# Sums over keys by block transposes on VectorE and one small matmul, in a two-layer graph network

## The chip, the cores and the metric

The kernel runs on one core of a Trainium2 chip, and the metric is the device time of that core in microseconds: the median of several executions. A core has five engines, each with its own queue of instructions, executed in order: TensorE (PE, the matrix multiplier; PEld in the profile is its loading of stationary operands), VectorE (DVE), ScalarE (ACT), GpSimd (POOL) and SyncE (SP), which issues the transfers to and from DRAM here. [...] PE writes to PSUM, of which the kernel keeps eight buffers of one bank each, and DVE and ACT empty them.

## The reference

Two layers over x of shape (64, 256, 512), in float32, with one adjacency matrix `adj` of 256 x 256.

```python
# layer 0: attention with 8 heads of 64, masked by adj
q = (x @ Wq + bq).reshape(b, n, H, HD)      # k and v alike
scores = einsum('bqhd,bkhd->bhqk', q, k) / sqrt(HD)
scores = scores + (1.0 - adj)[None, None, :, :] * -1e9
attn = softmax(scores, axis=-1)
out = einsum('bhqk,bkhd->bqhd', attn, v).reshape(b, n, d)
x = layernorm(x + out @ Wo + bo)
# layer 1: graph attention with one head
h = x @ W
s1, s2 = h @ a1, h @ a2
e = leaky_relu(s1[:, :, None] + s2[:, None, :], 0.2) * adj
att = softmax(e, axis=2)
x = layernorm(x + elu(att @ h + beta * h))
```

## The kernel before

The 64 batches are worked in 32 pairs. q, k and v of a pair are projected together, with seven products in place of eight (Strassen's scheme: `project`, whose matmuls all lie on line 437 and write the PSUM tiles `ps_chain`, `ps_cross`, `ps_second`, `ps_fourth` or `ps_pair`). The rest runs batch by batch; s = 0 or 1 is the batch in its pair. In the order of a batch the stages are:

- *scores*: for each of four head pairs c, four matmuls with 64 rows each into two PSUM tiles `ps_sc` (line 756). They hold keys on the partitions and queries along the row. DVE adds the mask (line 763), ACT takes the exponential without subtracting a maximum (765), giving `pT`, and POOL adds the two key halves into `both` (768).
- *sums*: the softmax denominators are sums over keys, thus over partitions. `denominators` does them with eight matmuls against a strip of ones into `ps_den` (781), takes the reciprocal on DVE (798), and lets ACT sum denominators and reciprocals into `range_sb` (794). The reciprocals go to DRAM as eight rows (806), and two transfers spread them over the partitions of `inv_all` (810).
- *mix*: the exponentials times v, into `ps_pv` (733). ACT copies it to `oT`, and DVE multiplies by `inv_all` (836).
- *o*: the output projection, added to x (914), with operands `oS` that POOL prepares (408); then the layer norm (569 to 586).
- *logits*: DVE's products with `wa_sb` (937), a small block transpose, a trip of one row through DRAM, and the masked softmax of layer 1 (966 to 986).
- *attention*, *spread*, *u*: the attention is transposed through DRAM and DVE (1003 to 1010), applied to the normed x (`X_sums`, `att_sums` prepared by POOL at 1046), the result `yT` (483) multiplied by W, then ELU (697 to 700), the second norm and the store (704).

Which stage of which pair PE works at when is written out by hand. `ROUND` is the order in one round, `LATER` says how many rounds after its own a stage of a pair comes, and `FINISH` is the order of the last stages. The class `Plan` takes all operations with assumed durations and dependences, gives PE's operations due times from that order (with `SWITCH` ns whenever the array's shape, `mode`, changes), and places the other engines' operations by greedy planning against those due times. What comes out is the fixed order of each engine's queue. `slots` says how many buffers of each kind there are.

At the end the check at line 1085 looks whether every value in `range_sb` is at most `SAFE` = 1e15. If not, a second, general path recomputes everything; with these inputs it isn't taken.

Of the kernel before, what the change touches and what calls it, by code (L numbers as in the profile page):

```python
# [22 lines left out]
ROUND = ("sums1", "mix1", "scores0", "spread1", "v", "u1", "attention0", "sums0", "mix0", "scores1", "o1", "x",  # L23
         "logits1", "q", "spread0", "o0", "attention1", "u0", "k", "logits0")

LATER = {"x": -2, "q": -1, "k": -1, "v": 0, "scores0": 0, "scores1": 0, "sums0": 0, "sums1": 1, "mix0": 0, "mix1": 1,
         "o0": 0, "o1": 1, "logits0": 0, "logits1": 1, "attention0": 1, "attention1": 1, "spread0": 1, "spread1": 2,
         "u0": 1, "u1": 2}

FINISH = (("sums1", 1), ("mix1", 1), ("scores0", 0), ("v", 0), ("attention0", 1), ("spread1", 2), ("sums0", 0), ("u1",  # L30
          2), ("mix0", 0), ("scores1", 0), ("o1", 1), ("logits1", 1), ("o0", 0), ("attention1", 1), ("u0", 1),
          ("spread1", 1), ("logits0", 0), ("spread0", 1), ("sums1", 0), ("mix1", 0), ("attention0", 0), ("spread0",
          0), ("o1", 0), ("attention1", 0), ("u1", 1), ("u0", 0), ("logits1", 0), ("spread1", 0), ("u1", 0))
# [25 lines left out]
class Plan:  # L59
# [11 lines left out]
    SWITCH = 250.0  # L71
# [161 lines left out]
def gnn_two_layers(ctx: ExitStack, tc: tile.TileContext, x, adj, Wq, bq, Wk, bk, Wv, bv, Wo, bo, W, a, beta, out):  # L233
# [13 lines left out]
    slots = {"xin": 2, "x": 4, "two": 6, "xP": 1, "piece": 6, "full": 4, "half": 18, "xS": 2, "st": 76, "ps": 8, "rows": 4, "svT": 4, "line": 4, "square": 4}  # L247
# [83 lines left out]
    range_sb = once([2, B], "range_sb")  # L331
# [348 lines left out]
    def batch(m, s, qT, kT, V, dram, general):  # L680
# [59 lines left out]
        def attention_by_keys():  # L740
# [3 lines left out]
            inv, everywhere = sb("half", [N], "inv"), sb("full", [C, N], "inv_all")  # L744
            rows = Buf(dram_pool, "rows", [H, N], "rows")

            def scores(c):

                turn("scores")
# [11 lines left out]
                for i in range(2):  # L761
# [5 lines left out]
                    if not last:  # L767
                        plan.op("POOL", 725, lambda h=h, i=i: nc.gpsimd.tensor_tensor(  # L768
                            both[c][:, i, :], pT[h][:, 0, :], pT[h][:, 1, :], ALU.add),
                            [pT[h]], [(both[c], i)])  # L770

            def denominators():
                turn("sums")

                acc = ps([N], "ps_den")

                def pe():
                    for k in range(NT if last else 1):
                        for i in range(2):
                            for c in range(C):  # L780
                                nc.tensor.matmul(  # L781
                                    acc[32 * c:32 * c + 32, :], ones[:, 16 - 16 * i:48 - 16 * i],
                                    pT[2 * c + i][:, k, :] if last else both[c][:, i, :],
                                    start=i == 0 and k == 0, stop=i == 1 and (k == NT - 1 or not last))

                if last:
                    plan.op("PE", 1500, pe, pT, [acc], mode="sums", claims=[inv])
                else:
                    plan.op("PE", 1000, pe, both, [acc], mode="sums", claims=[inv])

                def sum_of(i, src):

                    junk = sb("half", [N], "junk")
                    plan.op("ACT", 600, lambda: nc.scalar.activation(  # L794
                        junk[A], src[A], AF.Identity, accum_out=range_sb[:, i, b:b + 1]), [src],
                        [junk, (range_sb, (i, b))])

                plan.op("DVE", 1750, lambda: nc.vector.reciprocal(inv[A], acc[A]), [acc], [inv])  # L798
                for i, d in enumerate((acc, inv)):
                    sum_of(i, d)  # L800
                if last:
                    select = sb("half", [H, HD], "select")
                    plan.op("DVE", 690, lambda: nc.vector.tensor_copy(
                        select[A], ident[:, 0:P:P // H].unsqueeze(2).to_broadcast([P, H, HD])), [acc], [select])
                    return [spread_last(select, inv, g) for g in range(2)]
                plan.op("SP", 500, lambda: nc.sync.dma_start(rows[A], inv[0:P:P // H, :]), [inv], [rows])
                for i in range(2):
                    def spread(i=i):
                        r = rows[A]
                        nc.sync.dma_start(everywhere[i * HD:(i + 1) * HD], bass.AP(  # L810
                            tensor=r.tensor, offset=r.offset + i * N, ap=[[0, HD], [2 * N, C], [1, N]]))

                    plan.op("SP", 1000, spread, [rows], [(everywhere, i)])
# [29 lines left out]
            spread_inv = denominators()  # L843
# [3 lines left out]
        def attention_by_queries():  # L847
# [5 lines left out]
            def scores(t, g):  # L853
                turn("scores")
# [227 lines left out]
    fine, row, least = st(1, "fine"), ps([P], "row"), st(1, "least")  # L1082
    ok = sb("half", [2, B], "ok")

    def check():
        nc.vector.tensor_scalar(ok[A], range_sb[A], SAFE, None, ALU.is_le)
        nc.vector.tensor_reduce(fine[A], ok[A], AX.XY, ALU.min)

    plan.op("DVE", 500, check, [range_sb], [ok, fine])
# [53 lines left out]
```

## Time and profile before

| | |
|---|---|
| Time, median of 3 runs | 2719.87 us (2719.57 to 2720.87) |
| Span of the profiled execution, first to last instruction | 2718.3 us |
| Mean granted TensorE clock | 0.997 |
| Instructions | 47307 |
| A pair of batches in the middle (1033.98 to 1117.62) | 83.64 us |
| Transfers | 300.79 MB, 111 GB/s |

The profiled execution has a span of 2718.3 us; the runs that are timed are 1.6 us above that, for what lies around the span. In a line of the profile, L781 is line 781 of the kernel; `ps_den<-both,ones` is what is written and read; "x64 | 112.5, 1758 | 18.5" are the count, the busy time in microseconds, the mean length of one in nanoseconds, and the time that the engine stood idle just before these instructions. Lengths of instructions that follow each other overlap by their latencies, so their sum is above the busy time. A float32 matmul is recorded as two.

### The profile page before, as it was taken

What the parts mean: (1) busy time and instruction counts of PE and PEld (TensorE: products, weight loads), DVE (VectorE), ACT (ScalarE), POOL (GpSimd) and SP (SyncE); (2) the same over time, 40 slices, a digit from 0 to 9 for tenths busy, and PEclk for the clock granted to TensorE, in tenths of its full rate; (3) what the DMA queues carried; (4) which work ended last, traced back from release to release, by engine and by line L of the source; (5) the groups of instructions that cost most, each with busy time, mean ns of one, the idle gap of its engine ahead of it and who ended that gap; (6) DMA issues with size and microseconds to landing.
All of it is one profiled execution on the core that took longest, in us unless ns stands there. A gap on an engine that the chain in (4) does not pass through costs nothing.

```text
span 2718.3 us, 47307 instructions
## 1 busy us (share of the span) xinstructions
PE 2696.2 (99%) x15919; PEld 2268.6 (83%) x15919; DVE 1956.4 (72%) x3677; ACT 1548.9 (57%) x3713; POOL 1721.8 (63%) x2254
## 2 busy tenths in 40 slices
PE   9999999999999999999999999999999999999997
PEld 7888888888888888888888888888888888888886
DVE  6777677777777677777767777777767777776766
ACT  3455556556556565565555655655656556555566
POOL 5756666665666656666666666566665666666654
PEclk9999999999999999999999999999999999999998
DMA  8434434344443444434443434444344443443221
GB/s 245 103 100 123 121 96 117 96 121 125 99 121 86 119 129 106 106 104 105 125 119 98 115 95 125 125 98 120 88 120 129 106 107 104 104 126 103 83 70 45
DMA packets 579056, 300.79 MB, mean 111 GB/s; under 512 B 404864, under 2 KB 509816, under 8 KB 578808
## 3 DMA queue, kind: packets, MB, share of 16 engines
q1 hardware_dynamic: 578680, 297.68, 41.4%
q8 instruction: 130, 2.13, 0.3%
q14 instruction: 118, 0.97, 0.1%
q0 software_dynamic: 128, 0.01, 0.0%
HBM read 245.11 MB, written 52.48 MB: 109 GB/s over the span
## 4 chain that ended last, share of the span: by engine, by line
PE 97%; DVE 1%; POOL 0%; ACT 0%; issue 0%; DMA 0%; SPq 0%; ACTq 0%; POOLq 0%; DVEq 0%
PE ps_chain L437 33%; PE ps_cross L437 22%; PE ps_pair L437 10%; PE ps_sc L756 8%; PE ps_pv L733 8%; PE ps_second L437 6%; PE ps_fourth L437 6%; PE ps_den L781 2%; DVE junk L543 0%; DMA xin<-in_x_dram 0%; ACT junk L569 0%; DMA row<-line 0%; SPq L631 0%; PE ps_y L1021 0%; PE ps_plain L502 0%
## 5 line engine op out<-in xcount | busy, mean ns | idle before, releaser
L768 POOL TENSOR_TENSOR both<-pT 128x256 f32<-128x256 f32 x504 | 354.6, 731 | 383.1 <-ACT pT L765 383.1
L763 DVE TENSOR_TENSOR pT<-ps_sc,maskT_sb 128x512 f32<-128x512 f32 x512 | 324.0, 680 | 85.4 <-PE ps_sc L756 85.4
L765 ACT ACTIVATE pT<-pT 128x512 f32<-128x512 f32 x512 | 304.0, 625 | 52.3 <-DVE pT L763 49.7
L937 DVE SCALAR_TENSOR_TENSOR junk<-x,wa_sb 128x512 f32<-128x512 f32 x256 | 206.8, 833 | 109.4 <-ACT x L586 108.2
L756 PE MATMUL ps_sc<-qT,kT 64*128 64x256 f32 x2048 | 238.4, 382 | 0.0
L733 PE MATMUL ps_pv<-pT,v 128*64 128x256 f32 x2048 | 235.1, 382 | 0.0
L756 PEld LDWEIGHTS ps_sc<-qT,kT 64*128 64x128 f32 x2048 | 192.8, 187 | 44.4 <-issue 24.6
L474 ACT COPY u<-ps_chain 128x256 f32<-128x256 f32 x126 | 46.9, 372 | 318.4 <-PE ps_chain L437 318.2
L586 ACT ACTIVATE x<-x,nmr,rs 128x512 f32<-128x512 f32 x256 | 197.5, 808 | 44.7 <-POOL nmr L582 44.6
L733 PEld LDWEIGHTS ps_pv<-pT,v 128*64 128x64 f32 x2048 | 141.4, 137 | 91.0 <-DVE kT L483 12.8
L1046 POOL TENSOR_TENSOR X_sums<-x 128x256 f32<-128x256 f32 x126 | 151.6, 1213 | 100.1 <-ACT x L586 98.6
L569 ACT ACTIVATE junk<-x,mean 128x512 f32<-128x512 f32 x256 | 182.2, 714 | 3.8 <-DVE mean L575 3.6
L569 ACT ACTIVATE junk<-x 128x512 f32<-128x512 f32 x256 | 159.4, 625 | 38.6 <-DVE x L914 31.8
L717 POOL TENSOR_TENSOR x<-x,res_sb 128x512 f32<-128x512 f32 x128 | 175.7, 1374 | 0.0
L580 POOL TENSOR_SCALAR rs<-sq 128x2 f32<-128x2 f32 (+1 forms) x130 | 34.8, 268 | 208.8 <-ACT junk L569 203.5
L408 POOL TENSOR_TENSOR oS<-oT 128x256 f32<-128x256 f32 x126 | 92.2, 731 | 86.7 <-DVE mean L575 53.0
L836 DVE TENSOR_TENSOR oT<-oT,inv_all 128x512 f32<-128x512 f32 x126 | 132.7, 1091 | 0.0
L975 POOL TENSOR_TENSOR e<-e,adj_sb 128x512 f32<-128x512 f32 (+1 forms) x66 | 82.2, 1247 | 77.0 <-DVE e L972 77.0
L437 PE MATMUL ps_chain<-so_sb,oS 128*128 128x256 f32 x504 | 129.3, 379 | 0.0
L437 PE MATMUL ps_chain<-sw_sb,yS 128*128 128x256 f32 x504 | 129.2, 379 | 0.0
L798 DVE RECIPROCAL inv<-ps_den 128x256 f32<-128x256 f32 x64 | 112.5, 1758 | 18.5 <-ACT junk L794 9.3
L408 POOL TENSOR_TENSOR yS<-yT 128x256 f32<-128x256 f32 x126 | 91.8, 729 | 51.7 <-DVE yT L483 31.8
(242 smaller groups left out, 7162.7 us busy)
## 6 DMA issues: line engine op xcount, KB each, us to landing
x<-in_x_dram SPq DMA_DIRECT2D x64, 512.0 KB
out_dram<-x SPq DMA_DIRECT2D x128, 256.0 KB
inv_all<-rows SPq DMA_DIRECT2D x126, 256.0 KB
xin<-in_x_dram SPq DMA_DIRECT2D x248, 128.0 KB
wq_sums<-wq_sums SPq DMA_DIRECT2D x124, 256.0 KB
wk_sums<-wk_sums SPq DMA_DIRECT2D x124, 256.0 KB
wq_sums<-in_L_gnn_Wq_dram SPq DMA_DIRECT2D x93, 256.0 KB
wk_sums<-in_L_gnn_Wk_dram SPq DMA_DIRECT2D x93, 256.0 KB
```

Source lines behind the costliest of these rows:

```text
L408: plan.op("POOL", 180 + 545 * width // P, lambda: nc.gpsimd.tensor_tensor(dst(), p(), m(), ALU.subtract), reads, writes)
L437: nc.tensor.matmul(dst[:, f, :], lhs, rhs, start=start and f == 0 and c == 0, stop=c == inner - 1, skip_group_check=True)
L569: plan.op("ACT", 700, lambda: nc.scalar.activation(junk[A], X[:, t, :], func, bias=mean[:, i:i + 1] if bias else 0.0, accum_out=to[:, i:i ...
L586: plan.op("ACT", 810, lambda i=i, t=t: nc.scalar.activation(X[:, t, :], X[:, t, :], AF.Identity, bias=nm[:, i:i + 1], scale=rs[:, i:i + 1] ...
L717: plan.op("POOL", 1270, lambda t=t: nc.gpsimd.tensor_tensor(X[:, t, :], X[:, t, :], res_sb[A], ALU.add), [res_sb], tokens(t))
L733: nc.tensor.matmul(acc[r * HD:(r + 1) * HD, i, :], V[:, 2 * k + s, h * HD:(h + 1) * HD], pT[h][:, k, :], start=k == 0, stop=k == NT - 1)
L756: nc.tensor.matmul(acc[j][:, k, :], kT[r:r + HD, c, key_blk(k)], own(qT, r, c), start=True, stop=True)
L763: plan.op("DVE", 690, lambda h=h, i=i: nc.vector.tensor_add(pT[h][A], acc[i][A], maskT_sb[A]), [acc[i], maskT_sb], [pT[h]])
L765: plan.op("ACT", 620, lambda h=h: nc.scalar.activation(pT[h][A], pT[h][A], AF.Exp, scale=1.0 / HD ** 0.5), [pT[h]], [pT[h]])
L768: plan.op("POOL", 725, lambda h=h, i=i: nc.gpsimd.tensor_tensor(both[c][:, i, :], pT[h][:, 0, :], pT[h][:, 1, :], ALU.add), [pT[h]], [(bot ...
L937: plan.op("DVE", 780, lambda t=t, i=i, junk=junk: nc.vector.scalar_tensor_tensor(junk[A], X[:, t, :], 1.0, wa_sb[:, i, :], op0=ALU.mult, o ...
L1046: plan.op("POOL", ns, lambda: nc.gpsimd.tensor_tensor(dst(), p(), m(), op), reads, writes)
```

## The change

The sums over keys get another form in all batches but the last. `both[c]` (keys of one half on 128 partitions, two heads, 256 queries) is transposed on DVE in blocks of 32 x 32 into `flip`, and a reduction along 32 elements leaves in `part` the sum of each block of 32 keys, with the query modulo 32 on the partition. After the four head pairs, one matmul with `part` as the stationary operand (64 columns: 8 heads by 8 groups of 32 queries) and `fold_sb` (four unit matrices of 32 x 32 stacked, made once) as the moving one adds the four blocks of keys. It leaves the denominators as 64 x 32. Their reciprocals, now 32 columns instead of 256, go to one row of a DRAM tile `rows_all` that keeps all batches; the spreading transfers read from there.

ACT's two summing passes go, with `range_sb`. Instead the end reads `rows_all` back once and compares the reciprocals with `SAFE` and 1/`SAFE` in four passes on DVE. The last batch keeps the matmuls against ones and gets its own comparison.

`ROUND`, `LATER` and `FINISH` are written anew: sums now come after the mix, and the four head pairs of the scores are stages of their own. `SWITCH` becomes 100. There is one `half` buffer fewer, and `flip`, `part` and `inv` have one buffer each.

```diff
-ROUND = ("sums1", "mix1", "scores0", "spread1", "v", "u1", "attention0", "sums0", "mix0", "scores1", "o1", "x",
-         "logits1", "q", "spread0", "o0", "attention1", "u0", "k", "logits0")
+ROUND = ("mix1", "sums1", "scores30", "scores20", "scores00", "scores10", "logits0", "v", "spread1", "o1", "u1", "x",
+         "mix0", "sums0", "scores31", "scores21", "scores01", "scores11", "attention0", "q", "attention1", "logits1",
+         "k", "spread0", "o0", "u0")
...
-    SWITCH = 250.0
+    SWITCH = 100.0
...
-    slots = {"xin": 2, "x": 4, "two": 6, "xP": 1, "piece": 6, "full": 4, "half": 18, "xS": 2, "st": 76, "ps": 8, "rows": 4, "svT": 4, "line": 4, "square": 4}
+    slots = {"xin": 2, "x": 4, "two": 6, "xP": 1, "piece": 6, "full": 4, "half": 17, "flip": 1, "part": 1, "inv": 1,
+             "xS": 2, "st": 76, "ps": 8, "rows": 4, "svT": 4, "line": 4, "square": 4}
...
-    range_sb = once([2, B], "range_sb")
+    rows_all = Buf(dram_pool, "rows_all", [B - 1, H * N], "rows_all")
...
+    fold_sb = once([32], "fold_sb")
+    plan.op("DVE", 150, lambda: nc.vector.tensor_reduce(
+        fold_sb[A], ident.rearrange("p (b j) -> p j b", j=32), AX.X, ALU.add), [], [fold_sb])
...
-                turn("scores")
+                turn(f"scores{c}")
...
+                if last:
+                    return
+                turned = sb("flip", [2, N], "flip")
+                plan.op("DVE", 640, lambda: nc.vector.transpose(turned[A], both[c][A]), [both[c]], [turned])
+                plan.op("DVE", 600, lambda: nc.vector.tensor_reduce(
+                    part[:, 2 * c:2 * c + 2, :], turned[A].rearrange("p i (q k) -> p i q k", k=32), AX.X, ALU.add),
+                    [turned], [(part, c)])
...
+                acc, inv = ps([32], "ps_den"), sb("inv", [32], "inv")
+                plan.op("PE", 130, lambda: nc.tensor.matmul(
+                    acc[0:P // 2], part[A].rearrange("p h q -> p (h q)"), fold_sb[A], start=True,
+                    stop=True), [part, fold_sb], [acc], mode="columns", claims=[inv])
+                plan.op("DVE", 280, lambda: nc.vector.reciprocal(inv[0:P // 2], acc[0:P // 2]), [acc], [inv])
+                spread_rows(lambda r: r.rearrange("(p q) -> p q", q=32), lambda: inv[0:H * N // 32], inv)
+
+            def spread_rows(to, src, inv):
+                plan.op("SP", 500, lambda: nc.sync.dma_start(to(rows_all[b]), src()), [inv], [(rows_all, b)])
+                for i in range(2):
+                    def spread(i=i):
+                        r = rows_all[b]
+                        nc.sync.dma_start(everywhere[i * HD:(i + 1) * HD], bass.AP(
+                            tensor=r.tensor, offset=r.offset + i * N, ap=[[0, HD], [2 * N, C], [1, N]]))
+
+                    plan.op("SP", 1000, spread, [(rows_all, b)], [(everywhere, i)])
...
-                def sum_of(i, src):
-
-                    junk = sb("half", [N], "junk")
-                    plan.op("ACT", 600, lambda: nc.scalar.activation(
-                        junk[A], src[A], AF.Identity, accum_out=range_sb[:, i, b:b + 1]), [src],
-                        [junk, (range_sb, (i, b))])
...
+                def in_range():
+                    nc.vector.tensor_scalar(ok[:, 0, :], inv[A], SAFE, None, ALU.is_le)
+                    nc.vector.tensor_scalar(ok[:, 1, :], inv[A], 1.0 / SAFE, None, ALU.is_ge)
+                    nc.vector.tensor_reduce(last_ok[A], ok[A], AX.XY, ALU.min)
...
+    plan.op("SP", 1000, lambda: nc.sync.dma_start(
+        flat(kept), bass.AP(tensor=rows_all[A].tensor, offset=rows_all[A].offset, ap=[[n, P], [1, n]])), [rows_all],
+        [kept])
...
+        nc.vector.tensor_scalar(flat(ok), flat(kept), SAFE, None, ALU.is_le)
+        nc.vector.tensor_scalar(flat(kept), flat(kept), 1.0 / SAFE, None, ALU.is_ge)
+        nc.vector.tensor_tensor(flat(ok), flat(ok), flat(kept), ALU.mult)
+        nc.vector.tensor_reduce(fine[:, 0:1], flat(ok), AX.X, ALU.min)
+        nc.vector.tensor_tensor(fine[:, 1:2], fine[:, 0:1], last_ok[A], ALU.mult)
```

In the instruction order that the planner makes of this, each round on PE is: mix and sum, scores, v, spread, o, u; then mix and sum, scores, q, k, spread, o, u. Before, it was: sum, mix, scores, spread, v, u; then sum, mix, scores, o, q, spread, o, u, k.

## The prediction

> **What bounds the kernel now.** I read four views, in the order in which one rules the next out. First the profile's page: the engines' busy time and the chain that ended last.
>
> ```profile
> span 2718.3 us, 47307 instructions
> PE 2696.2 (99%) x15919; PEld 2268.6 (83%) x15919; DVE 1956.4 (72%) x3677; ACT 1548.9 (57%) x3713; POOL 1721.8 (63%) x2254
> PE 97%; DVE 1%; POOL 0%; ACT 0%; issue 0%; DMA 0%; SPq 0%; ACTq 0%; POOLq 0%; DVEq 0%
> ```
>
> TensorE (PE) is 99% of the span and 97% of the chain. A busy PE could still be a slow PE, so I read the waits of PE next (microseconds in total, times, longest).
>
> ```profile
> PE tr_x L620 <- DMA xin<-in_x_dram: 4.3, 2, 3.7
> PE ps_chain L437 <- ACT attT L999: 1.5, 1, 1.5
> PE tr_a L996 <- DVE rc L983: 1.4, 1, 1.4
> ```
>
> These are the largest, and all lie in the first or the last 50 us. Between them PE waits for nobody. So a microsecond taken from PE's queue comes off the end one for one, and work on another engine is free until it makes PE wait. Third, PE's timeline around one sum over keys (start, length, line, count):
>
> ```profile
> 1115.68 1.03 PE L437 MATMUL ps_chain<-sw_sb,yS 128*128 128x256 f32 x4
> 1116.64 1.07 PE L781 MATMUL ps_den<-both,ones 128*32 128x256 f32 x16
> 1117.64 3.67 PE L733 MATMUL ps_pv<-pT,v 128*64 128x256 f32 x32
> 1121.25 3.73 PE L756 MATMUL ps_sc<-qT,kT 64*128 64x256 f32 x32
> 1124.90 1.13 PE L437 MATMUL ps_chain<-wo_sb,oT 128*128 128x256 f32 x4
> ```
>
> Lengths overlap, so I use starts. The sum L781 holds PE from 1116.64 to 1117.64: 1.00 us. Four full-size products are 0.864 us apart elsewhere, so 1115.68 + 0.864 = 1116.54: the change of array shape before the sum costs 0.10 us. Fourth, the sum over one pair of batches, in the stretch view (length, then busy time of PE, PEld, DVE, ACT, POOL):
>
> ```profile
> core 0: us, PE busy (x) PEld busy (x) DVE busy (x) ACT busy (x) POOL busy (x), PEclk, DMA share, GB/s
> 1033.98:1117.62 83.64, 83.64 (x500) 70.61 (x496) 60.64 (x114) 48.28 (x117) 53.68 (x70) 1.00 0.44 112
> ```
>
> A pair takes 83.64 us, all of it PE at full clock, with DVE (VectorE) at 60.6.
>
> **The change, part by part.**
>
> *The sum on PE.* Its 8 matmuls leave 63 of 64 batches: 63 x 1.00 = 63.0 us. In their place stands one matmul with 64 stationary columns and 32 moving ones. The trace shows none so small. It shows every f32 matmul as two instructions (1008 in 63 x 8), and these weight loads:
>
> ```profile
> L733 PEld LDWEIGHTS ps_pv<-pT,v 128*64 128x64 f32 x2048 | 141.4, 137 | 91.0 <-DVE kT L483 12.8 <-issue 12.7 <-DVE v L483 0.8
> L756 PEld LDWEIGHTS ps_sc<-qT,kT 64*128 64x128 f32 x2048 | 192.8, 187 | 44.4 <-issue 24.6
> ```
>
> Nothing hides a load of 64 columns behind a multiply of 32, so the nearest row gives 2 x 137 = 274 ns. The Trainium skill (TensorE: Matmul & The Clock Gate, section "LDWEIGHTS (loading the stationary operand)") prices a load by its columns alone, P/1.2 ns: 53 ns, twice 107. The rows explain the gap: 64 to 128 columns cost 50 ns more, 0.8 a column, as the rule says, over a fixed 85 ns which the rule leaves out. By the row the sum is 63 x (1.00 - 0.274) = 45.7 us saved, by the rule 56.3. The fixed part is mostly overlapped in streams (128-column products follow each other at 0.11 us though their loads last longer), so I take 0.15, nearer the rule: 63 x 0.85 = **53.6 us saved**.
>
> *Shape changes.* Before: full, sum, mix, scores, full: four changes. After, the instruction order is mix, sum, scores in every round, and a 64-column output has the mix's shape: three. The change that goes is already inside the 1.00 us; the 0.10 in front stays, now in front of the mix. No further credit. The planner's SWITCH of 100 instead of 250 and the new ROUND only set this order.
>
> *ScalarE.* Two summing passes a batch go (383 + 194 + 417 + 192 ns, 76 us in all) from an engine at 57% that PE never waits for: nothing. POOL's work stays.
>
> *VectorE.* Mean rows that bear on it:
>
> ```profile
> L798 DVE RECIPROCAL inv<-ps_den 128x256 f32<-128x256 f32 x64 | 112.5, 1758 | 18.5 <-ACT junk L794 9.3 <-PE ps_den L781 9.2
> L1010 DVE STREAM_TRANSPOSE attT<-att_b 128x512 f32<-128x512 f32 x62 | 43.5, 702 | 0.1
> L977 DVE TENSOR_REDUCE nm<-e 128x2 f32<-128x512 f32 x62 | 41.9, 675 | 1.1 <-POOL e L975 1.1
> L836 DVE TENSOR_TENSOR oT<-oT,inv_all 128x512 f32<-128x512 f32 x126 | 132.7, 1091 | 0.0
> ```
>
> Added per batch: 4 transposes and 4 reductions of 128x512, 4 x (0.702 + 0.675) = 5.5 us. Removed: 1.76 of reciprocal, which on 32 columns costs some 0.35 (from 165 ns at 2 columns, 6.3 ns each more). Net +4.1 a batch, +8.2 a pair: DVE goes from 60.6 to 68.8 of about 81.9 us. This is hidden only while DVE, whose queue is in order, clears PSUM and the operands in time, so I walk the tighter half of the new order: scores, v, spread, o, u, mix, sum, about 35 us on PE (the half with q and k has 47). Products' lengths come from starts in PE's timeline: v 12.10, spread 3.15, o and u 6.05 each. DVE's instructions there, at mean durations: masks 8 x 0.68, new ones 5.5, v adds 4 x 0.68, logits 3 x 0.91, the two L836 2.2, transpose 0.7, adds for y, x, u 16 x 0.42, rest (logits' softmax, ELU, statistics) 8.8: 34.8 us. Queued instructions overlap by 7% (16 masks of 680 ns take 10.1 us in a pair): 32.4, or 93% of the half. Tight, but not over.
>
> Walk, t = 0 at the scores: PE has v from 3.75 to 15.85, spread to 19.0, o to 25. DVE: reciprocal, transpose, eight masks with one add between to 6.9; transpose and reduction to 8.1 (the transpose waits for POOL's sums of two exponentials, whose masks are done at 4.5; 0.6 on ScalarE and 2 x 0.73 on POOL make 6.6, in time); waits for v's third product (9.1); v add, logits, to 11.5; L836 twice to 13.7; v add, transpose, reduction, transpose to 16.3; two v adds to 17.6; the y add at 17.95. PE's sixth spread product (18.1) waits for that add: a slack of about 0.1 us. In o a similar place comes out 0.1 late. Each late moment shifts PE and gives DVE the time back, so I take 0.15 us a pair, 31 pairs: **5 us lost**, from 0 to the case below. L836 is what moves it: behind it in the queue stand the v adds, and for them PE.
>
> *Reciprocals through DRAM.* The same 8 KB a batch in 64 pieces of 128 B instead of 8 of 1 KB; the two spreading transfers are the same, and on SP's queue they follow the write at once in one half as before (1119.59 to 1121.47), in the other they stand between weight fetches. In the tight half L836 comes 11.5 us after the sum. Reciprocal 0.45, write to the end of the spread's issue 3.2 as before (1119.59 to 1122.76), and landing at most 4.5 (in one half issued by 1099.94, with L836 at 1104.48): 8.2, hidden. Without that cover L836 waits, and behind it the v adds, for which PE's banks wait. SBUF has one `half` buffer fewer; 0.
>
> *End.* The range check is now one 516 KB read on SP between the last spread and the last batches' logit and attention transfers, which need their data only a round later, then four passes of 1008 columns on DVE: by slopes between 256 and 512 columns 2 x 0.72 + 1.19 + 1.18 + 0.3 = 4.1 us, plus 1.4 for the last batch's own. They stand ahead of the two copies of the last y, for which the last projection waits. DVE has holes there (3.9 us at 2680): between 0 and 5.5, I take **2 us lost**.
>
> Sum: 2718.3 - 53.6 + 5 + 2 = 2671.7 us of span. The runs' median is 1.6 above the span (2719.87 against 2718.3), the same program frame around it: **2673 us**.
>
> **Rivals.**
>
> *A, nothing is lost:* the small matmul costs the rule's 0.107, the two other terms are 0. 2718.3 - 56.3 + 1.6 = 2663.6. For it: PE never waited for DVE in a round. Against: 93%. Chance 0.17, 2655 to 2667.
>
> *B, POOL holds DVE up:* The Trainium skill (SBUF — State Buffer, section "SBUF: two separate sides") says a DVE instruction with two SBUF inputs and a POOL instruction exclude each other for their whole length. The new transposes and reductions have one input, and their rows are steady (673 to 711 ns), but L836 has two: median 684, mean 1091, longest 1761. Mean price: my walk. With both at the longest, the y add is 1.3 us later, in every pair: 31 x 1.3 = 40 us, 2718.3 - 53.6 + 40 + 2 + 1.6 = 2708. For it: the round repeats, so a collision repeats. Against: the median is the free one. Chance 0.19, 2684 to 2714.
>
> *C, DVE becomes the bound (slower):* one mechanism, DVE's queue in the tight half (scores to sum). Without overlap (34.8), with both L836 at the longest and the waits for PE in the walk (3), it lasts 39.1 against 35: 4.1 a pair, 127 us, 2795. It decides from (53.6 - 2)/31 = 1.7 us a pair. Against: it needs all of DVE's instructions at their dearest. Chance 0.04.
>
> *D, the small matmul is no gain:* if it drained the array on both sides and so cost as much as the eight, 1 us, with nothing else lost: 2720. Against: it has the mix's shape, and measured shape changes are 0.10. Chance 0.02.
>
> **The numbers.** My forecast, 0.58, has its own range 2662 to 2684. The wide range, 2658 to 2698, holds it, most of A and half of B. A measurement tells 0.2% (5.4 us). Faster: forecast, A and B, and of C the little below 1.7 us a pair: 0.95; same, most of D: 0.015; slower, the rest of C and D: 0.035.
>
> **What would show it.** The sum's start to the scores' start after the mix: mix 3.6 plus 0.15. A pair at 82 us; PE waits for DVE in spread or o of 0 to 0.3 us a pair; DVE near 83% of the span; the last products a few us after where their work alone would put them. I am wrong if the small matmul takes over 0.3 us, if PE waits on v's or y's adds by more than 0.5 us a pair, or if the end waits for the range check.

## The result, and the profile after

The kernel after takes 2688.94 us (median of 4 runs, 2687.40 to 2692.57) against 2719.90 us for the kernel before beside it. The ratio is 0.9889 with a 95% interval of 0.9875 to 0.9903: faster by 1.1%. The forecast was 2673.0, so the sign was right, the wide range held it, and 16 of the expected 47 us did not come. It fell outside the likeliest case's own range (2662 to 2684) and into the band of rival B. The profiled execution was the slowest of the four (2692.57; span 2690.8), 27.5 us of span below the one of before.

The page of the kernel after: engines and the chain that ended last.

```profile
span 2690.8 us, 45707 instructions
PE 2662.2 (99%) x15037; PEld 2252.2 (84%) x15037; DVE 2212.4 (82%) x4188; ACT 1483.6 (55%) x3457; POOL 1688.5 (63%) x2254
PE 97%; DVE 1%; DMA 0%; issue 0%; ACT 0%; POOL 0%; SPq 0%; POOLq 0%; DVEq 0%
```

PE is still 99% of the span. DVE rose from 72% to 82%. The time at PE's own place is seen in its timeline around the new small matmul (start, length, line, count), and the cost of a pair of batches in the stretch view, the whole pair first and then its two halves, the one with v and the one with q and k.

```profile
1111.11 1.13 PE L448 MATMUL ps_chain<-sw_sb,yS 128*128 128x256 f32 x4
1112.17 3.67 PE L744 MATMUL ps_pv<-pT,v 128*64 128x256 f32 x32
1115.67 0.25 PE L794 MATMUL ps_den<-fold_sb,part 128*64 128x32 f32 x2
1115.85 1.35 PE L767 MATMUL ps_sc<-qT,kT 64*128 64x256 f32 x10
```

```profile
1080.18:1162.80 82.62, 82.55 (x471) 70.07 (x469) 68.51 (x132) 46.24 (x108) 52.47 (x71) 1.00 0.42 112
1080.18:1115.85 35.67, 35.60 (x208) 29.59 (x206) 31.49 (x60) 20.01 (x47) 26.62 (x34) 1.00 0.17 49
1115.85:1162.80 46.95, 46.95 (x265) 40.48 (x263) 37.02 (x73) 26.23 (x62) 25.85 (x37) 1.00 0.62 161
```

From the start of the mix to the start of the scores it is 1115.85 - 1112.17 = 3.68 us. Before, the mix alone took 1121.25 - 1117.64 = 3.61 at the place shown, and 3.60 in the mean of 62 such places. So the small matmul adds 0.08 us, and each batch saves 0.92 where the eight matmuls took 1.00. Two batches should bring the pair from 83.64 to 81.80. It takes 82.62: 0.82 us of each pair is lost again.

Where? The list of PE's waits does not say; its largest lines lie in the first and last 130 us. The weight loads (PEld) have three lines that repeat some 29 times, once a pair, with at most 0.4 us each; in the kernel before none of them stands more than twice (total, times, longest; PE's largest lines first):

```profile
PE tr_x L631 <- DMA xin<-in_x_dram: 5.4, 3, 3.7
PE tr_s L975 <- DVE junk L959: 3.0, 2, 2.3
PE ps_sc L767 <- DVE kT L494: 1.4, 1, 1.4
```

```profile
PEld ps_pair L448 <- POOL yS L419: 12.5, 28, 0.4
PEld ps_chain L448 <- ACT u L485: 11.5, 29, 0.4
PEld ps_cross L448 <- ACT u L485: 10.8, 29, 0.4
```

PE itself shows as busy (82.55 of 82.62), because the record of a matmul that starts late is only longer. Starts tell it. In PE's timeline an undisturbed product follows the one before by 0.864 us; in the half with v, *o* has steps of 1.10 and 0.94 (0.31 lost) and *u* has 1.01, 0.96, 1.03 and, to the mix, 1.06, which is 0.96 where nothing waits (0.51 lost). Together 0.82. The half with q and k has no such step. The timeline over these two places, with lines left out at the dots:

```profile
1102.62 1.03 PE L448 MATMUL ps_cross<-so_sb,oT 128*128 128x256 f32 x4
1102.82 0.42 DVE L936 TENSOR_TENSOR x<-x,ps_chain 128x256 f32<-128x256 f32 x1 [0.17 <-PE ps_chain L448]
1103.16 0.41 DVE L936 TENSOR_TENSOR x<-x,ps_pair 128x256 f32<-128x256 f32 x1
...
1103.72 1.10 PE L448 MATMUL ps_pair<-wo_sb,oS 128*128 128x256 f32 x4
...
1104.62 1.27 POOL L419 TENSOR_TENSOR xS<-xT,xS 128x512 f32<-128x512 f32 x1
...
1105.20 1.24 DVE L959 SCALAR_TENSOR_TENSOR junk<-x,wa_sb 128x512 f32<-128x512 f32 x1
...
1105.85 3.00 POOL L728 TENSOR_TENSOR x<-x,res_sb 128x512 f32<-128x512 f32 x2
...
1106.48 1.24 DVE L988 TENSOR_SCALAR z<-row,s 128x256 f32<-128x256 f32 x1
...
1107.64 0.74 DVE L936 TENSOR_TENSOR x<-x,ps_chain 128x256 f32<-128x256 f32 x2
...
1108.08 0.63 ACT L580 ACTIVATE junk<-x 128x512 f32<-128x512 f32 x1 [1.12 <-DVE x L936]
1108.11 1.03 PE L448 MATMUL ps_chain<-sw_sb,yS 128*128 128x256 f32 x4
...
1108.71 0.35 ACT L485 COPY u<-ps_cross 128x256 f32<-128x256 f32 x1
...
1109.12 0.70 PE L448 MATMUL ps_cross<-sw_sb,yT 128*128 128x256 f32 x2
```

Two readings offer themselves. (Products are numbered as in `project`, which issues them in the order 1, 5, 2, 6, 3, 4, 7.) In o, the fourth product goes into `ps_pair` and starts at 1103.72, just after DVE has read the second product out of it (1103.16 to 1103.57); that read stands in DVE's queue behind an add that waited for a later product. In u, POOL adds the bias to x (L728, two instructions, 3.00 us). Meanwhile DVE's small row add L988, 336 ns at its fastest, takes 1.24 us. DVE's last x adds start at 1107.64. ACT's norm of x waits for them until 1108.08, and the copy of `u<-ps_cross`, behind it in ACT's in-order queue, frees its PSUM tile only at 1109.06. PE goes on at 1109.12. The product of the logits just before, L959, is long as well: 1.24 us, where 0.68 is its fastest. Whether DVE's new work, POOL, or the new order is to blame is what the experiments had to tell.

### The profile page after: what moved, and what is told of

Its sections match the earlier page's. It is cut to its first block, busy times and chain, and to the rows that moved or that the text cites. A ratio compares the mean times of both kernels' runs of the same rounds, so it can differ in the third digit from the quotient of the medians.

```text
span 2690.8 us, 45707 instructions
## 1 busy us (share of the span) xinstructions
PE 2662.2 (99%) x15037; PEld 2252.2 (84%) x15037; DVE 2212.4 (82%) x4188; ACT 1483.6 (55%) x3457; POOL 1688.5 (63%) x2254
## 4 chain that ended last, share of the span: by engine, by line
PE 97%; DVE 1%; DMA 0%; issue 0%; ACT 0%; POOL 0%; SPq 0%; POOLq 0%; DVEq 0%
PE ps_chain L448 34%; PE ps_cross L448 22%; PE ps_pair L448 10%; PE ps_sc L767 9%; PE ps_pv L744 8%; PE ps_second L448 6%; PE ps_fourth L448 6%; PE ps_plain L513 0%; DMA xin<-in_x_dram 0%; DVE junk L959 0%; DMA row<-line 0%; PE ps_den L794 0%; DVE junk L554 0%; DVE x L711 0%; PE ps_plain L508 0%
## 5 line engine op out<-in xcount | busy, mean ns | idle before, releaser
L779 POOL TENSOR_TENSOR both<-pT 128x256 f32<-128x256 f32 x504 | 382.6, 786 | 76.8 <-ACT pT L776 74.6
L774 DVE TENSOR_TENSOR pT<-ps_sc,maskT_sb 128x512 f32<-128x512 f32 x512 | 318.3, 676 | 22.3 <-PE ps_sc L767 22.3
L776 ACT ACTIVATE pT<-pT 128x512 f32<-128x512 f32 x512 | 294.1, 624 | 30.9 <-DVE pT L774 30.8
L591 POOL TENSOR_SCALAR rs<-sq 128x2 f32<-128x2 f32 (+1 forms) x130 | 26.2, 202 | 404.8 <-ACT junk L580 402.2
L959 DVE SCALAR_TENSOR_TENSOR junk<-x,wa_sb 128x512 f32<-128x512 f32 x256 | 213.8, 862 | 37.6 <-ACT x L597 36.6
L785 DVE STREAM_TRANSPOSE flip<-both 128x512 f32<-128x512 f32 x252 | 174.9, 694 | 4.4 <-DVE part L786 0.5
L786 DVE TENSOR_REDUCE part<-flip 128x16 f32<-128x512 f32 x252 | 172.1, 683 | 6.5
L728 POOL TENSOR_TENSOR x<-x,res_sb 128x512 f32<-128x512 f32 x128 | 177.3, 1406 | 0.0
L488 ACT ACTIVATE kT<-ps_chain,bk_sb 128x256 f32<-128x256 f32 x128 | 53.8, 472 | 168.6 <-PE ps_chain L448 168.6
L1068 POOL TENSOR_TENSOR att_sums<-attT 128x128 f32<-128x128 f32 x126 | 70.7, 561 | 120.2 <-DVE attT L1032 114.4
L936 DVE TENSOR_TENSOR x<-x,ps_chain 128x256 f32<-128x256 f32 x252 | 100.2, 417 | 38.0 <-PE ps_chain L448 32.2
```

What stands on the lines that cost most here:

```text
L728: plan.op("POOL", 1270, lambda t=t: nc.gpsimd.tensor_tensor(X[:, t, :], X[:, t, :], res_sb[A], ALU.add), [res_sb], tokens(t))
L774: plan.op("DVE", 690, lambda h=h, i=i: nc.vector.tensor_add(pT[h][A], acc[i][A], maskT_sb[A]), [acc[i], maskT_sb], [pT[h]])
L776: plan.op("ACT", 620, lambda h=h: nc.scalar.activation(pT[h][A], pT[h][A], AF.Exp, scale=1.0 / HD ** 0.5), [pT[h]], [pT[h]])
L785: plan.op("DVE", 640, lambda: nc.vector.transpose(turned[A], both[c][A]), [both[c]], [turned])
L786: plan.op("DVE", 600, lambda: nc.vector.tensor_reduce(part[:, 2 * c:2 * c + 2, :], turned[A].rearrange("p i (q k) -> p i q k", k=32), AX.X ...
L959: plan.op("DVE", 780, lambda t=t, i=i, junk=junk: nc.vector.scalar_tensor_tensor(junk[A], X[:, t, :], 1.0, wa_sb[:, i, :], op0=ALU.mult, o ...
```

## The experiments

One thing must be known to read them. The planner fixes every queue from assumed durations, so an edit that changes an operation's planned price, or takes it out, rearranges all queues. I read each run in two pieces: a pair of batches in the steady rounds, and the end, from the scores of the last pair to the end of the span, where the planner is free (121.2 us before, 123.5 after).

### Does the gain come from the sums alone, and the loss from the new order?

The old order with the new sums, `SWITCH` and buffers:

```diff
-ROUND = ("mix1", "sums1", "scores30", "scores20", ... )   LATER, FINISH of the kernel after
+ROUND = ("sums1", "mix1", "scores0", "spread1", "v", "u1", "attention0", ... )   those of the kernel before
-                turn(f"scores{c}")
+                turn("scores")
```

> The changed kernel with the order lists (ROUND, LATER, FINISH) of the kernel before; the new sums, SWITCH and buffers stay. A pair of the changed kernel takes 82.62 us, and its PE work without gaps is 81.8. Theory 1 (VectorE is late in the half round with v, spread, o, u, and PE waits for it): the old order puts v into a half of only some 29 us with nearly the same VectorE work, so gaps stay or grow: 2690 to 2715. Rival (the new order itself costs the lost 0.8 us a pair): no gaps in the old order, 2663 to 2672.

2683.15 us (ratio 0.9866, 0.9850 to 0.9883): between what the two expected, and not told apart from the kernel after in total. By pieces it is plain. The stretch view of one pair in this run:

```profile
1346.96:1428.82 81.86, 81.86 (x470) 72.01 (x469) 65.27 (x131) 46.49 (x108) 52.62 (x70) 1.00 0.43 113
```

The pair lost next to nothing: 81.86. With the same sums and the same DVE instructions, the old order needs 0.76 us a pair less than the new one. So the change of the sums without the new order is worth 1.78 us a pair, and the new order costs something in the rounds. (DVE's busy time is 65.27 us here against 68.51: the same instructions are shorter in this order, above all the row add that is L988 in the kernel after, 1.72 us a pair for 3.87.) But the end of this run lasts 133.8 us, with waits such as these of PE, and gives some 10 us back:

```profile
PE ps_cross L444 <- POOL yT L415: 5.1, 2, 4.1
...
PE ps_cross L444 <- ACT yT L481: 3.0, 2, 1.8
PE ps_chain L444 <- ACT attT L1017: 2.4, 1, 2.4
```

### Three edits that rearranged the queues

The transposes and reductions taken out. One tiny operation stands for them, at a planned price of 100; the sums over keys are left out:

```diff
-                turned = sb("flip", [2, N], "flip")
-                plan.op("DVE", 640, ... nc.vector.transpose(turned[A], both[c][A]) ...)
-                plan.op("DVE", 600, ... nc.vector.tensor_reduce(part[...], turned[A] ...) ...)
+                plan.op("DVE", 100, lambda: nc.vector.tensor_scalar(
+                    part[:, 2 * c:2 * c + 2, :], both[c][:, :, 0:N // 32], 1.0, None, ALU.add), [both[c]], [(part, c)])
```

> The changed kernel without the eight transposes and eight reductions per pair: part is filled by one small VectorE instruction from a corner of both, so the denominators are not the sums over keys. Takes some 10 us of VectorE work from a pair; PE, ScalarE, POOL and transfers as in the changed kernel. Theory 1 (VectorE late): the gaps on PE go, a pair takes 81.8 us and the time is 2658 to 2665. Rival (POOL or ScalarE late on their own account): a pair stays at 82.4 to 82.6 and the time above 2680.

2705.17 us (0.9943, 0.9927 to 0.9960): slower than the kernel after by 16 us with less work. The rival's "above 2680" holds, but neither theory had it slower. The pair is 82.72, the end 136.4. The rearranged DVE queue put an x add later (a wait `ps_pair` for DVE's L933, 29 times, 8.8 us). The run says nothing about DVE's load; it says that less work can be planned worse.

POOL's bias add left out:

```diff
-        for t in range(NT):
-            plan.op("POOL", 1270, lambda t=t: nc.gpsimd.tensor_tensor(X[:, t, :], X[:, t, :], res_sb[A], ALU.add),
-                    [res_sb], tokens(t))
```

> The changed kernel without POOL's two adds of the residual bias per batch (1.4 us each, the longest of its queue); the bias is left out. Theory 2 (in the o and u stages VectorE's logit products and additions of the row are held up by these POOL adds, 1.24 us in place of 0.65; then x is late, ScalarE's norm starts late, and u's copies stand behind it): the gaps in u go, 0.4 to 0.5 us a pair, 2670 to 2678. Theory 1 without the hold-up (VectorE simply has too much to do): under 0.15 us a pair, 2684 to 2690.

2679.97 us (0.9850, 0.9833 to 0.9866): between the two expectations, nearer that of the second theory. The pair falls to 82.08, the end grows to 127.6. It speaks for POOL, but in rearranged queues.

The row add L988 moved from DVE to ACT:

```diff
-            plan.op("DVE", 480, lambda t=t: nc.vector.tensor_scalar(
-                z[:, t, :], row[A], sv[:, t, 1:2], None, ALU.add), ...
+            plan.op("ACT", 480, lambda t=t: nc.scalar.activation(
+                z[:, t, :], row[A], AF.Identity, bias=sv[:, t, 1:2]), ...
```

> The changed kernel with the addition of the row in the logits (four instructions a pair, 0.35 us free and up to 1.24 held up) on ScalarE instead of VectorE. Theory 1 and 2: VectorE gains 1.5 to 2.5 us a pair and the gaps shrink by half or more: 2668 to 2680. Rival (ScalarE's queue is what is late in u): four more instructions of 0.5 us in that queue make the gaps longer, 2690 to 2700.

2693.11 us (0.9902, 0.9886 to 0.9919). The total is where the rival expected it, but for another reason: the pair did fall, to 82.23, and the end took it back with 133.8. After these three I changed only what an operation does, at an unchanged planned price, so that every queue keeps its order.

### DVE's work or POOL's hold-up, in unchanged queues

First DVE's new work made small. The sums over keys are left out:

```diff
-                ... nc.vector.transpose(turned[A], both[c][A]) ...
+                ... nc.vector.transpose(turned[:, :, 0:32], both[c][:, :, 0:32]) ...
-                ... nc.vector.tensor_reduce(part[:, 2 * c:2 * c + 2, :], turned[A].rearrange(...), AX.X, ALU.add) ...
+                ... nc.vector.tensor_scalar(part[:, 2 * c:2 * c + 2, :], turned[:, :, 0:N // 32], 1.0, None, ALU.add) ...
```

> The kernel after, every queue in exactly its order, but each transpose flips only the first 64 of its 512 columns and each reduction over keys is replaced by a copy of 16 columns plus 1 (the sums over keys are left out). About 0.55 us of VectorE work goes from each of the two kinds of instruction, some 130 to 150 us in the whole run, 4.2 to 4.6 us a pair. Theory D (VectorE's added work is what makes TensorE wait, 0.83 us a pair between the sums): the pair falls from 82.62 to 81.8-82.0 us and the time to 2662-2672 us. Theory P (the waits come from POOL's bias adds holding VectorE up, whatever else is in its queue): most of the waits stay, pair 82.3-82.6, time 2678-2689 us.

2690.28 us (0.9889, 0.9873 to 0.9906): no change, and just above the range of theory P too. A pair in the stretch view:

```profile
1078.38:1161.04 82.66, 82.57 (x471) 70.07 (x469) 61.70 (x132) 46.25 (x108) 52.48 (x71) 1.00 0.44 112
```

DVE has 6.8 us less in the pair (61.70 against 68.51), and the pair lasts as long. Theory D is dead: it is not the amount of DVE's added work that makes PE wait.

Then POOL's bias add made small (it takes 16 of 512 columns; the rest of the bias is left out):

```diff
-            ... nc.gpsimd.tensor_tensor(X[:, t, :], X[:, t, :], res_sb[A], ALU.add) ...
+            ... nc.gpsimd.tensor_tensor(X[:, t, 0:16], X[:, t, 0:16], res_sb[:, 0:16], ALU.add) ...
```

> The kernel after, every queue in exactly its order, but POOL's addition of the bias to x takes 16 of the 512 columns (the rest of the bias is left out). 128 instructions shrink from 1.41 us to a few tenths. Theory P (POOL's bias add holds VectorE's two operations before the u projection up): the two gaps at u go, 0.4-0.5 us a pair, the 0.3 us in o stays: pair 82.1-82.2, time 2672-2677 us. Theory D (VectorE's own added work): no more than 0.1 us a pair, time 2685-2689 us.

2671.63 us (0.9821, 0.9804 to 0.9837), at the lower edge of what theory P expected, 17.3 us below the kernel after; the pair is 82.11. The same place in its timeline:

```profile
1099.24 0.85 POOL L728 TENSOR_TENSOR x<-x,res_sb 128x16 f32<-128x16 f32 x2
...
1099.88 0.36 DVE L988 TENSOR_SCALAR z<-row,s 128x256 f32<-128x256 f32 x1
...
1100.16 0.74 DVE L936 TENSOR_TENSOR x<-x,ps_chain 128x256 f32<-128x256 f32 x2
...
1101.23 0.35 ACT L485 COPY u<-ps_cross 128x256 f32<-128x256 f32 x1
...
1101.51 1.03 PE L448 MATMUL ps_chain<-sw_sb,yS 128*128 128x256 f32 x4
...
1102.37 0.59 PE L448 MATMUL ps_cross<-sw_sb,yT 128*128 128x256 f32 x2
```

L988 takes 0.36, the ACT copy ends at 1101.58, 0.8 us before PE writes the tile again, and PE's step is 1102.37 - 1101.51 = 0.86: the gap at u is gone. The two lines `PEld ... <- ACT u` are gone from the list of waits; the line `ps_pair <- POOL yS` is still there with 12.4 us.

If POOL excludes DVE for an instruction at a time, shorter instructions should do as well as fewer columns. The same add as two halves, nothing left out:

```diff
-            ... nc.gpsimd.tensor_tensor(X[:, t, :], X[:, t, :], res_sb[A], ALU.add) ...
+            ... [nc.gpsimd.tensor_tensor(X[:, t, half(i)], X[:, t, half(i)], res_sb[:, half(i)], ALU.add) for i in range(2)] ...
```

> The kernel after, every queue in the same order, with POOL's bias add of 512 columns issued as two of 256 columns; nothing is left out. POOL's time for it stays about the same (0.73 us for 256 columns by the row of oS, so 2.9 us for a batch). If VectorE is held up for as long as the one POOL instruction takes that it meets, its row add before the u projection is held for 0.7 us in place of 1.24, its last x adds come 0.4-0.5 us sooner and most of the gap at u goes: 0.3-0.5 us a pair, time 2673-2680 us. If VectorE is held up for as long as POOL has such work at all, nothing is gained: 2686-2691 us.

2674.55 us (0.9834, 0.9818 to 0.9851), as expected if the hold is one instruction long, 14.4 us below the kernel after with the same work done. The pair is 82.11, the same as with the small add; the 2.9 us between these two runs lie in the end (118.6 us there, 122.0 here). The row add in the view of one tile (count: shortest/median/longest in ns), in the kernel before, in the kernel after, with the small bias add, and with the halves:

```profile
L966 DVE TENSOR_SCALAR z<-row,s x124: 341/353/915, 106.8 to 2656.5; 128x256 f32<-128x256 f32 x124
```

```profile
L988 DVE TENSOR_SCALAR z<-row,s x124: 336/1070/1432, 126.3 to 2615.8; 128x256 f32<-128x256 f32 x124
```

```profile
L988 DVE TENSOR_SCALAR z<-row,s x124: 336/360/882, 125.8 to 2600.1; 128x256 f32<-128x256 f32 x124
```

```profile
L988 DVE TENSOR_SCALAR z<-row,s x124: 335/691/892, 125.1 to 2599.4; 128x256 f32<-128x256 f32 x124
```

The hold lasts about one POOL instruction: the median goes from 1070 to 691 ns, though POOL spends slightly more in all on the four halves (3.29 us) than on the two whole ones (3.00). The trace of the kernel after shows the hold itself: 74 of the row adds in the rounds meet a bias add and outlast it, and each of them ends 148 to 154 ns after a bias add ends.

### The other gap, in o

In VectorE's queue, the add that reads the second product out of `ps_pair` put ahead of the add that waits for the sixth, after planning, all else in place:

```diff
+            at = len(plan.ops)
             project(left["o"], right_o, False, [], onto, onto)
+            adds = [n for n in range(at, len(plan.ops)) if plan.ops[n][0] == "DVE"]
+            ahead.append((adds[2], adds[3]))
...
     order = plan.place()
+    for pair_add, chain_add in ahead:
+        at, chain_at = order.index(pair_add), order.index(chain_add)
+        if chain_at < at:
+            order.insert(chain_at, order.pop(at))
```

> The kernel after, in which VectorE's x add from ps_pair (second product of o) is put ahead of the x add from ps_chain (sixth product) in VectorE's queue, in every batch where it stood behind it; all else stays in its place. Theory: the 0.3 us gap in o comes from this order, since TensorE may not write the fourth product into ps_pair before VectorE has read the second out of it, and that read stands behind one that waits for a later product: pair 82.62 to 82.3, time 2678-2682 us. Rival, the releaser that the trace names for the weight load there (POOL's yS): nothing changes, 2686-2691 us.

2686.45 us (0.9882, 0.9865 to 0.9898): hardly a gain, pair 82.61. That is the number of the rival, but not for its reason, as the timeline says.

```profile
1099.45 1.03 PE L449 MATMUL ps_cross<-so_sb,oT 128*128 128x256 f32 x4
1100.32 1.03 PE L449 MATMUL ps_pair<-wo_sb,oS 128*128 128x256 f32 x4
...
1101.44 1.27 POOL L420 TENSOR_TENSOR xS<-xT,xS 128x512 f32<-128x512 f32 x1
...
1101.72 1.54 DVE L963 SCALAR_TENSOR_TENSOR junk<-x,wa_sb 128x512 f32<-128x512 f32 x1
...
1104.63 1.03 PE L449 MATMUL ps_chain<-sw_sb,yS 128*128 128x256 f32 x4
1105.93 0.48 PE L449 MATMUL ps_cross<-sw_sb,yT 128*128 128x256 f32 x1 [0.27 <-ACT u L486]
```

The gap in o is gone (1100.32 - 1099.45 = 0.87), so its cause was the order of the two adds and not POOL's `yS`, which the trace named as releaser. But PE, now 0.3 us earlier, meets the copy of `u<-ps_cross` later by as much: that step is 1.30 where it was 1.01. The two waits do not add up; taking the first away lengthens the second. The trace shows what keeps the chain behind that copy late. The product of the logits (L963, L959 in the kernel after) now starts 0.3 us earlier against POOL's preparation of `xS`, and is 0.3 us longer, 1.54 for 1.24. In all 29 rounds of either run it ends some 0.55 us after this POOL instruction ends. So POOL holds DVE here too, with another instruction than the bias add. No run makes that one shorter.

Both edits together:

> Both edits together, the bias add in halves and the ps_pair add ahead, nothing left out. If the two gaps are all that is lost between the sums, the pair comes to 81.8-82.0 us (gap-free it would be 81.79) and the time to 2664-2671 us. If taking one gap away makes the next one wider, as far as 82.2-82.4 and 2676-2684 us.

2670.96 us (0.9821, 0.9805 to 0.9837): the time is just inside the first expectation, the pair just outside it. The pair is 82.06, so the second edit adds 0.05 to the first, not 0.3. What is left sits again in u (`PEld ps_chain <- ACT u`, 28 times, 11.1 us): ACT's copies stand behind the norm's passes, the norm behind DVE's x adds, and these behind the product L963, 1.55 us long here beside `xS`. What that product's hold costs by itself is not shown.

### The price of the small matmul

Issued five times in place of once, each overwriting the last:

```diff
-                    stop=True), [part, fold_sb], [acc], ...
+                    stop=True) for _ in range(5)], [part, fold_sb], [acc], ...
```

> The kernel after, every queue in the same order, with the small matmul of the sums issued five times in place of once (each overwrites the last; nothing is left out). 63 times 4 more of it prices it: at 0.07 us each, which is what the one adds between mix and scores in the trace of after, +18 us, 2705-2710; at the 0.15 us of the prediction, +38 us, 2724-2730; at its recorded duration of 0.19 us, +48 us, 2734-2740.

2717.18 us (0.9989, 0.9981 to 0.9998). 28.2 us more for 63 x 4 = 252 matmuls is 0.112 us each, between the first two expectations (whose 0.07 is the 0.08 above, read at one place). In its records a pass takes 223 ns and a load 138 (shortest/median/longest), while ten passes fit between 1174.31 and 1174.95, 64 ns each:

```profile
L794 PE MATMUL ps_den<-fold_sb,part x630: 192/223/243, 58.9 to 2622.6; 128*64 128x32 f32 x158
```

```profile
L794 PEld LDWEIGHTS ps_den<-fold_sb,part x630: 133/138/138, 58.7 to 2622.6; 128*64 128x64 f32 x158
```

```profile
1174.31 0.72 PE L794 MATMUL ps_den<-fold_sb,part 128*64 128x32 f32 x10
1174.95 1.35 PE L767 MATMUL ps_sc<-qT,kT 64*128 64x256 f32 x10
```

### The range check at the end

Its four passes cut from 1008 to 16 columns (the check of the other columns is left out):

```diff
-    def flat(t):
-        return t[A].rearrange("p c n -> p (c n)")[:, 0:n]
+    def flat(t, w=16):
+        return t[A].rearrange("p c n -> p (c n)")[:, 0:w]
```

> The kernel after, every queue in the same order, in which the four passes of the range check at the end read 16 of their 1008 columns (the check of the other columns is left out; the read from DRAM stays whole). If the check costs the end what the prediction took for it, 2 us go: 2686-2688 us. If VectorE's holes hide it but for the 0.3 us wait that the trace shows: 2688-2690 us. At the upper bound of the prediction, 5.5 us: 2683 us.

2688.05 us (0.9882, 0.9866 to 0.9899): on the border of the first two expectations, 0.9 us below the kernel after, not told apart from it. In the kernel after, PE waits 0.31 us for the check (`row<-ident,fine`, start 2670.62). The profiled ends agree: 119.8 us here, and 120.2 and 121.1 in the two runs with the check whole that moved the pair add and repeated the small matmul.

### An end for the old order

The old order of the rounds, with another order for the end that was searched on the planner's own figures (`FINISH` anew, `OPEN`, the number of freely placed PE operations, 80 for 70), nothing left out:

```diff
-FINISH = (("sums1", 1), ("mix1", 1), ("scores0", 0), ("v", 0), ("attention0", 1), ("spread1", 2), ... )
+FINISH = (("mix1", 1), ("sums1", 1), ("scores10", 0), ("scores20", 0), ("scores00", 0), ("scores30", 0), ("v", 0),
+          ("spread1", 2), ("attention0", 1), ("sums0", 0), ("u1", 2), ("scores01", 0), ("o1", 1), ... )
-    OPEN = 70
+    OPEN = 80
```

> The order of before in the rounds (81.86 us a pair with the new sums, no gaps, by the run with the old order), the sums by transposes, and a newly searched order for the end, which the planner puts 12 us shorter than that of before; nothing is left out. If the end comes out as planned: 2668-2675 us. If the freely planned end is as long on the chip as in the run with the old order (133.8 us after the last scores of a round), or longer: 2680-2690 us.

2671.38 us (0.9822, 0.9806 to 0.9838), as expected if the end came out as planned: pair 81.86, end 123.3 instead of 133.8. So there are two ways to 2671, both 0.7% below the kernel after: the new order with POOL's add in halves and the pair add first, or the old order with the new sums and a fitting end.

## Why the prediction was right or wrong

**The small matmul: right in kind, priced too high.** I took 0.15 us; in place it adds 0.08, so the 63 batches save 58.0 us and not 53.6. Repeated, it costs 0.112 each. The bound from the row (0.274, two recorded loads end to end) is refuted. The rule of the Trainium skill (TensorE: Matmul & The Clock Gate, section "LDWEIGHTS (loading the stationary operand)"), whose 107 ns I had as the other bound, is near what the repeated one shows. My sentence that nothing hides a load behind so short a multiply failed: recorded lengths of 138 and 223 ns overlap down to 64 ns a pass, and in place the first load lies beside the mix's last multiply (0.21 us ahead of the first pass).

**VectorE's load: the sum right, the conclusion wrong.** DVE was to rise to 68.8 us a pair and measures 68.51; the half with v was to be 93% loaded and is 31.49 of 35.67, 88%. That the sum came out so near is in part luck: hold-ups by POOL grew at one line (L988) and shrank at another (L858), and in the old order the same instructions take 65.27. But the step "PE waits for DVE, 0.15 us a pair, 5 us lost" failed: 0.82 us a pair is lost, 25 us if all 31 pairs lost as much. And it does not come from the load: 6.8 us of DVE work less a pair changed nothing. This is the term of the sum that was mis-sized, and it explains more than the whole miss of 16 us. The matmul's price, taken too high, hid 4 us of it.

**Where PE waits.** The walk put the tight place at the sixth spread product (slack 0.1) and a second one in o, "0.1 late". The spread has no gap; the place in o is the right one, with 0.31. I had walked the queue by mean durations, with DVE's adds in the order of the products. The planner put the read of `ps_pair` behind the one of `ps_chain`. By the code it knows of no wait for it: two products share one PSUM tile, and in the plan only the producer of the first half is a dependence of the second. The places in u, 0.51, I had not walked: there the wait goes from POOL over DVE and ACT's queue to PE, and I had looked for DVE's own adds only.

**Rival B: the mechanism, not the place.** It had 0.19, and its band holds the result. Making POOL's add small, or splitting it, took 0.51 of the 0.82 us off each pair, so more than half of the loss is POOL's bias add holding DVE up. But I had priced it at L836, the two-input product with `inv_all`. That one became freer: its mean fell from 1091 ns to 810 (L858). Held up were L988, which has one SBUF input and a scalar, and ahead of it L959, which has two. The page that rival B named (the Trainium skill, SBUF — State Buffer, section "SBUF: two separate sides") counts DVE instructions in a two-port mode too; I had kept only the two-input ones. The runs agree as far as they can: L988 takes 336 ns from SBUF, 475 ns when the same operation reads its row from PSUM (in the last batches), and has a median of 1070 in the kernel after. That it runs in such a mode, no run shows directly. In the kernel before this row's mean was 566; there the bias adds of a batch stood apart from each other (1060.92 and 1066.43, say), here they stand back to back just where L988 comes. Rivals A (nothing lost), C (DVE as the bound) and D (no gain from the small matmul) did not come true; A's price for the matmul, 0.107, is near what its repetition shows.

**The end.** 2 us for the range check was inside its bounds and is more than it costs: about 1 us, too little to be told from none. The end as a whole is 2.3 us longer than before in the profiled execution, much of which is chance by the other ends of the same order (119.8 to 122.3 us).

**The sum.** From the scores of the third pair (170.83 before, 171.44 after) to those of the last pair, 29 pairs: 29 x (83.66 - 82.62) = 30.4 us gained, made of 53.4 saved and 23 lost; 0.6 lost at the start and 2.3 at the end give the 27.5 of span. The other five batches with the new sums lie in the start and the end and should have saved 4.6 us there, so some 7.5 us are lost in these two, where I had put 2. The rest to the 31.0 of the medians is that the profiled execution lay above the median of its four, so by the median some 4 are lost there. What they go to was not traced, but for the 0.3 us of the check. Of what I had named as showing me wrong, little came true: the small matmul is below 0.3 and the end does wait, 0.3 us, for the check; but PE's waits for x adds and u copies were not on my list. That the time still fell inside the wide range was the room given to rival B, and not the walk.

## What to carry to other kernels

When work is added to a half-idle engine, its share of the time says little: follow, for each PSUM tile that the bottleneck writes again, who must read it first and what stands ahead of that reader in its in-order queue, over two engines if need be. Where DVE must be on time beside a long POOL instruction, try splitting that one: here two halves brought the median of the held-up add from 1070 to 691 ns and the kernel from 2688.9 to 2674.6 us. And where a planner orders the queues, test a cause by shrinking the operation at an unchanged planned price; removing it makes a different program.

## What the runs showed of the hardware that I had not expected

A DVE add of 128x256 with a single SBUF tensor as input is held up by POOL, as two-input ones are: 336 ns at its fastest, a median of 1070 where POOL's bias adds take 1.4 us each, 691 where they are halved. A float32 matmul with 64 stationary and 32 moving columns, recorded at 138 ns of load and 223 ns of multiply for each of its two passes, costs 0.112 us in a row of its kind and 0.08 between two stages of other work. And PE's gaps of 0.08 to 0.24 us a product do not stand in its own list of waits here, but only with the weight loads, at times under a releaser that is not the cause: 12.5 us stood under POOL's `yS`, and moving one DVE add removed them.
